# A sum of two matrix blocks moved from VectorE to two DMA transfers, and earlier places for an eigensolver's products

## The chip, the core and the metric

The kernel runs on one core of one Trainium2 chip. The core has five engines with a queue each: TensorE (PE, matrix products, with its weight loads shown as PEld), VectorE (DVE), ScalarE (ACT), GpSimd (POOL) and SyncE (SP). In the kernel before, nearly all DMA transfers are issued from SP and a few from ACT; none is issued from GpSimd. The metric is the device time of one execution in microseconds (us); lower is better.

## The reference, cut to what matters

The program is a stack of four graph layers on an input of 8192 rows of 256 numbers (128 graphs of 64 nodes), all in float32, each with a residual and a layer norm. Two of them matter here.

```python
# layer 0: three graph convolutions with one 64x64 matrix (adj * S, and S is adj)
def _slconv(x, adj, S, W):
    support = jnp.einsum('bnf,fh->bnh', x, W)
    weighting = adj * S
    return jnp.einsum('nm,bmh->bnh', weighting, support)
h = relu(_slconv(x, adj, S, W1))      # W1: 256 x 512
h = relu(_slconv(h, adj, S, W2))      # W2: 512 x 1024
y = _slconv(h, adj, S, W3)            # W3: 1024 x 256

# layer 1: needs the eigenvectors of a 64x64 Laplacian
_, U = jnp.linalg.eigh(L_norm)
agg = jnp.einsum('mn,bnd->bmd', U.T, features)
```

Layers 2 (LSTMs over windows of nodes) and 3 (attention) follow; the change does not touch them.

## The kernel before, in words

**Two stages.** In the first, `layer0` (line 1116) runs layer 0 over 16 groups of four row tiles (512 rows). In the same stretch `eigen` (line 275) finds the eigenvectors of the one 64x64 Laplacian. In the second stage a planner (`Plan`, line 104) lays out layers 1 to 3. Layer 1 needs the eigenvectors, in the tiles `u2` and `ut2`, so no product of the second stage can start before `eigen` has ended.

**Products by Strassen's way.** The second and third weights' products are made of 2x2 blocks with seven products in place of eight (`seven`, line 1056; it yields after each product). The order of the products is 1, 2, 6, 5, 7, 3, 4. For the third weight the inputs are the four blocks `H11`, `H12`, `H21`, `H22` of the tile `h2` (each 128 partitions x 4 x 256 numbers, 512 KB) and sums of them (lines 998 and 999): product 1 reads `H11`, product 2 reads `H12`, product 6 reads `sh[:, 1]`, product 5 reads `sh[:, 0]`, product 7 reads the new `H21`, product 3 reads the new `H12`, and product 4 reads `H22`. Four operations of VectorE make the sums (lines 1141, 1142, 1147 and 1148): `sh[:, 0]` is `H21 + H22`; `sh[:, 1]` is that less `H11`; then `H21` and `H12` are overwritten. In the program they stand behind product 2. Between product 2 and product 6 stand four products of the next group with the first weight (`weigh`, line 1091, called for t = 0 to 3), which do not need the sums; the last group has none, since no group follows.

**An order written out by hand.** PE, DVE and ACT take their instructions in the order in which the program gives them (the `manual_schedule` at line 1161); SP's and POOL's are placed by the framework. The eigensolver is a generator that is advanced between products of layer 0 (`between`, line 953). It has a clock of its own: `now` counts what PE has been given (in `mm`, line 963, some 0.22 us for a product with 128 columns, 0.43 with 256, 0.86 with 512), and `Timed` (line 42) adds up what VectorE has been given in `free`: 0.25 us for an instruction and 0.0009 us for each element of a partition beyond 64. Layer 0's own sums go through the same clock, by `VL` (line 1001). The eigensolver yields the time at which it wants to go on. There are two such times:

```python
def soon():
    return max(free[0], until[0]) - 0.45
def full(turns=0):
    return max(free[0], until[0]) + 0.3 + 0.6 * turns
```

Ahead of vector work it waits for `soon`, ahead of a product on PE for `full`; `until` is when the product before will be there (0.5 us after it was given, line 314). What is not yet given when layer 0 ends is given at once behind it (lines 1169 to 1171).

**What the eigensolver does.** It reduces the matrix to tridiagonal form in 62 Householder steps (lines 382 to 448), each with one product on PE (`mm(pq, L, AQ)`, line 415) behind a `full`; it finds the eigenvalues by bisection (lines 562 to 593), the vectors by recursions (lines 603 to 641), and then turns them, fixes their signs and multiplies (lines 642 to 752), with seven further places behind a `full` or a wait of that kind, each the start of a chain PE, DVE, PE.

**Around the change.** Product results are added by DVE or copied by ACT one product later (`step`, line 1005). The layer norm of a group is made in pieces in the next group (`scalar_norm`, line 800), with three small POOL instructions to each half, and is then stored by a 512 KB transfer from SP (line 1105). When the second weight `aw2` and the third, `aw3`, have been read for the last time, the weights of the later layers are loaded in their places from SP (lines 878 and 1203).

Of the kernel before, what the change touches and what calls it, by code (L numbers as in the profile page):

```python
# [13 lines left out]
ALU = mybir.AluOpType  # L14
# [260 lines left out]
def eigen(tc, stack, a, ident, cst, u2, ut2, now, free):  # L275
# [9 lines left out]
    nc = tc.nc  # L285
    until = [0.0]
# [6 lines left out]
    def sb(shape, tag):  # L293
        uid[0] += 1
        return wp.tile(shape, F32, tag=tag, name=f"{tag}_{uid[0]}")
# [10 lines left out]
        return max(free[0], until[0]) - 0.45  # L306

    def full(turns=0):
        return max(free[0], until[0]) + 0.3 + 0.6 * turns

    def mm(out, lhsT, rhs):
        PE.matmul(out, lhsT, rhs, start=True, stop=True)  # L312
# [37 lines left out]
    V.tensor_scalar(dm, C["eye"], y, None, op0=ALU.mult)  # L350
    pm = ps([N, N], "pa")
    yield full(4)
    mm(pm, m, dm)

# [9 lines left out]
    A, QT = AQ[:N, 0, :], AQ[:N, 1, :]  # L364
    S.copy(LV[0][:N, 1, :], eye[:, 0:1].to_broadcast([N, N]))
    yield full()


# [13 lines left out]
    for i in range(N - 2):  # L382
# [16 lines left out]
        for update in late[1:]:  # L399
# [11 lines left out]
                               op1=ALU.mult, accum_out=v)  # L411
        V.tensor_copy(L[:N, 0, :], v.to_broadcast([N, N]))
        yield full()
        pq = ps([W, 2, N], "pa")
        mm(pq, L, AQ)
# [187 lines left out]
    for k in range(1, N):  # L603
        c = N - 1 - k
        t = sb([W, 1], "tw")
# [223 lines left out]
def kernel(  # L829
# [25 lines left out]
    nc = tc.nc  # L855
# [32 lines left out]
    def rows_of(g):  # L888

        return X[:, 4 * g:4 * g + 4, :] if g < RING else XA[:, 4 * (g - RING):4 * (g - RING) + 4, :]  # L890
# [99 lines left out]
    sh = pa.tile([P, 2, 4, 256], F32, name="sh")  # L990
    s3 = pa.tile([P, 4, D], F32, name="s3")
    A11, A12, A21, A22 = (m2[:, k:k + 2, r:r + 256] for r in (0, 256) for k in (0, 2))
    H11, H12, H21, H22 = (h2[:, c:c + 4, r:r + 256] for r in (0, 256) for c in (0, 4))
# [6 lines left out]
    free = [0.0]  # L1000
    VL = Timed(V, free, now)
# [3 lines left out]
    def step(then=None):  # L1005

        while pending:
            pending.pop(0)()
        if then:
            pending.append(then)  # L1010
        if norms:
            norms.pop(0)()
# [4 lines left out]
    def sums_of_weights(w, b12):  # L1017
        VL.tensor_sub(w[7], w[3], b12)
        VL.tensor_sub(w[5], b12, w[1])
        VL.tensor_sub(w[6], w[3], w[5])  # L1020
        VL.tensor_sub(w[4], w[2], w[6])

    def burst(dst, src, c):
        to = dst.rearrange("p c (t h n) -> p h c t n", h=2, n=N)
        p = [bank().rearrange("p (c t n) -> p c t n", c=2, t=4) for _ in range(2)]
        for t in range(4):
            for k in range(2):
                for m, f, h, hs in quads(c + k):
                    PE.matmul(p[h][m, k, t, :], src[hs, t, f], sqT2[hs, hs], start=True, stop=True)  # L1029
        now[0] += QUADS  # L1030
        between()

        def result():
            for h in range(2):
                S.copy(to[:, h, c:c + 2], p[h])  # L1035

        step(result)
# [6 lines left out]
    def by_second(j):  # L1044

        def product(out, i, new):
            w, a = (x[i] for x in second)
            chained(out, [[(w[:, k, c * P:(c + 1) * P], a[:, k, :]) for k in range(2)] for c in (2 * j, 2 * j + 1)], new)

        return product  # L1050
# [5 lines left out]
    def seven(n, product, c11, c12, c21, c22, last):  # L1056

        def view(b):
            return b[:, :2 * n].rearrange("p (i n) -> p i n", i=2)

        def add(dst, b):
            VL.tensor_add(dst, dst, b)
            if last is relu:
                relu(dst, dst)

        ch = view(bank("ch"))
        product(ch, 1, True)
        step(lambda: S.copy(c11, ch))
        yield
        b2 = view(bank())  # L1070
        product(b2, 2, True)
        step(lambda: add(c11, b2))
        yield
        product(ch, 6, False)
        step(lambda: S.copy(c12, ch))
        yield
        b5 = view(bank("b5"))
        product(b5, 5, True)
        step(lambda: S.copy(c22, b5))
        yield  # L1080
        product(ch, 7, False)
        step(lambda: add(c22, ch))
        yield
        product(b5, 3, False)
        step(lambda: add(c12, b5))
        yield
        product(ch, 4, False)
        step(lambda: last(c21, ch))
        yield

    def weigh(t):
        p = bank()
        run(p, [(m1[:, k, t * P:(t + 1) * P], aw1[:, k, :]) for k in range(2)])
        step(lambda: relu(h1[:, t, :], p))

    def mix_rows(g, t):
        p = bank().rearrange("p (t f) -> p t f", t=2)
        mm(p, sqT2, s3[:, t:t + 2, :])

        def result():  # L1100
            x2 = rows_of(order[g])[:, t:t + 2, :]
            VL.tensor_add(x2, p, x2)
            norms.extend(scalar_norm(tc, small, x2, half, spare))
            if t and order[g] >= RING:
                norms.append(lambda: nc.sync.dma_start(rest[order[g]], rows_of(order[g])))

        step(result)

    def sums_second():
        S1, S2, S4 = (ss[:, i] for i in range(3))  # L1110
        VL.tensor_add(S1, A21, A22)
        VL.tensor_sub(S2, S1, A11)
        VL.tensor_sub(A21, A11, A21)
        VL.tensor_sub(S4, A12, S2)

    def layer0():
        n = NT // 4
        burst(m1, rows_of(order[0]), 0)
        step()
        for t in range(4):  # L1120
            weigh(t)
        step()
        sums_of_weights(second[0], B12)
        for c in (0, 2):
            burst(m2, h1, c)
        step()
        for g in range(n):
            sums_second()
            for j in range(2):
                q = [h2[:, 4 * c + 2 * j:4 * c + 2 * j + 2, r:r + 256] for r in (0, 256) for c in (0, 1)]  # L1130
                for _ in seven(256, by_second(j), *q, relu):
                    pass
                if j == 0 and g + 1 < n:
                    burst(m1, rows_of(order[g + 1]), 0)
                if j == g == 0:
                    sums_of_weights(third[0], D12)
            q = [s3[:, r:r + 2, c:c + P] for r in (0, 2) for c in (0, P)]
            w3 = seven(P, by_third, *q, S.copy)
            next(w3)
            next(w3)  # L1140
            VL.tensor_add(sh[:, 0], H21, H22)
            VL.tensor_sub(sh[:, 1], sh[:, 0], H11)
            for t in range(4):
                if g + 1 < n:
                    weigh(t)
                if t == 0:
                    VL.tensor_sub(H21, H11, H21)
                    VL.tensor_sub(H12, H12, sh[:, 1])
            for _ in range(4):
                next(w3)  # L1150
            if g + 1 < n:
                burst(m2, h1, 0)
            next(w3)
            if g + 1 < n:
                burst(m2, h1, 2)
            for t in (0, 2):
                mix_rows(g, t)
        step()

    eig.extend([0.0, eigen(tc, phase_a, adst[:N, :], ident, eig_c, u2, ut2, now, free)])  # L1160
    with tc.manual_schedule(engines={mybir.EngineType.PE, mybir.EngineType.DVE, mybir.EngineType.Activation}):
        pt = bank()
        PE.transpose(pt[:N, :P], adst, ident)
        for h in range(2):
            hs = slice(h * N, (h + 1) * N)
            V.tensor_copy(adT2[hs, hs], pt[:N, hs])
        V.tensor_mul(sqT2, adT2, adT2)
        layer0()
        while eig:
            now[0] = max(now[0], eig[0])  # L1170
            between()
# [562 lines left out]
```

## Time and profile before

| | |
|---|---|
| time, 3 runs | 2320.1 us median (2317.26, 2320.21, 2320.1) |
| the profiled execution's own time | 2317.55 us |
| its span, first to last instruction | 2315.7 us |
| PE / PEld / DVE / ACT / POOL busy over the span | 97% / 86% / 75% / 52% / 6% |
| first stage | 0 to some 845 us, the second from there |
| one group of layer 0, from one to the next | 50.5 us |
| the four sums of one group on DVE | 1.21 us (three of them) and 1.22 us |

Times in the trace are counted from the span's first instruction. A row of the timeline gives the start, the busy time, the engine, the line, the operation, what it writes and reads (out<-in), and how many instructions were merged in it; in brackets stands how long the engine sat idle before it and what ended the wait. Names of tiles are cut at a digit: `h` is `h1` or `h2`, `m` is `m1` or `m2`, `aw` is any of the first layer's weights. L52 is the line in `Timed` that gives the eigensolver's vector instructions and layer 0's own, L964 is `mm` of layer 0, L312 that of the eigensolver, L162 the planner's. PE carries a float32 product as two records, so that eight products count x16. A row of a table of windows gives the stretch, its length, each engine's busy time with its number of instructions, the granted clock of PE as a share of full speed, the busy share of the DMA engines, and GB/s. Ends of products are modelled, and overlap with the next one's start.

### The profile page before, as it was taken

The numbers are of one execution on the slowest core, as the hardware profiler recorded it, in microseconds if no ns is written. First come the engines' busy times: TensorE is split into PE (matmuls) and PEld (weight loads), VectorE is DVE, ScalarE is ACT, GpSimd is POOL, SyncE is SP. The second block draws the span as 40 slices with busy tenths as digits, with TensorE's granted clock in tenths as the row PEclk, the third lists the DMA queues.
The fourth block names the chain that finished last, engine by engine and source line by source line (L and its number), as shares of the span: only waits on it lengthen the run. The fifth ranks groups of instructions, "written<-read, shape, count | busy, mean of one in ns | idle before, by whom it ended". The sixth has DMA issues, their size and how long they took to land.

```text
span 2315.7 us, 51333 instructions
## 1 busy us (share of the span) xinstructions
PE 2247.0 (97%) x20228; PEld 1988.2 (86%) x20228; DVE 1744.2 (75%) x5718; ACT 1200.2 (52%) x2896; POOL 137.8 (6%) x315
## 2 busy tenths in 40 slices
PE   8999999999999969999999999999999999999996
PEld 6788888878888858999999999899899899998895
DVE  5887877777888978665957967867867776868764
ACT  3444444443444425665656655555655655655654
POOL 0000000000000010000100100100000010000001
PEclk9999999999999989999999999999999999999998
DMA  7000000000000031000201221211211220312300
GB/s 241 11 10 11 10 11 12 18 10 10 11 10 1 13 124 43 20 1 19 87 27 47 76 65 40 76 67 47 76 56 49 67 74 23 112 58 92 99 19 19
DMA packets 80114, 107.88 MB, mean 47 GB/s; under 512 B 23296, under 2 KB 64256, under 8 KB 79872
## 3 DMA queue, kind: packets, MB, share of 16 engines
q1 hardware_dynamic: 79520, 104.32, 14.1%
q8 instruction: 159, 2.61, 0.5%
q14 instruction: 83, 0.68, 0.1%
q10 hardware_dynamic: 352, 0.28, 0.0%
HBM read 57.64 MB, written 45.09 MB: 44 GB/s over the span
## 4 chain that ended last, share of the span: by engine, by line
PE 87%; DVE 8%; issue 1%; ACT 1%; DMA 1%; POOL 1%; SPq 0%; ACTq 0%; DVEq 0%; POOLq 0%
PE ps L162 55%; PE ch L964 13%; PE ps L964 9%; PE b L964 7%; PE ps L1029 2%; DVE X L162 1%; DVE w L162 1%; PE pa L312 1%; POOL rs L162 1%; DVE st L162 1%; DVE D L52 1%; DVE gates L162 1%; DVE tw L52 1%; ACT gates L162 1%; DVE w L52 0%
## 5 line engine op out<-in xcount | busy, mean ns | idle before, releaser
L162 PE MATMUL ps<-w,wih 128*128 128x128 f32 (+2 forms) x2944 | 572.9, 298 | 5.5 <-DVE gates L162 4.9
L162 PEld LDWEIGHTS ps<-w,wih 128*128 128x128 f32 x2944 | 454.5, 191 | 39.8 <-issue 13.5
L162 PE MATMUL ps<-w,sums 128*128 128x128 f32 (+2 forms) x3104 | 476.9, 294 | 5.8 <-DVE w L162 5.2
L162 PEld LDWEIGHTS ps<-w,sums 128*128 128x128 f32 x3104 | 419.8, 191 | 23.4 <-DVE w L162 6.6
L162 ACT ACTIVATE gates<-gates,cbi 128x256 f32<-128x256 f32 (+4 forms) x736 | 315.7, 482 | 189.1 <-DVE gates L162 186.3
L162 DVE TENSOR_TENSOR gates<-gates,ps 128x512 f32<-128x512 f32 (+4 forms) x408 | 236.7, 585 | 190.3 <-PE ps L162 182.0
L162 ACT COPY gates<-ps 128x512 f32<-128x512 f32 (+4 forms) x408 | 205.7, 509 | 238.7 <-PE ps L162 233.4
L162 PE MATMUL ps<-hs,whh 128*128 128x128 f32 (+1 forms) x896 | 182.2, 285 | 2.3 <-DVE hs L162 2.3
L162 PE MATMUL ps<-w,whh 128*128 128x128 f32 (+1 forms) x896 | 181.1, 284 | 0.0
L162 PEld LDWEIGHTS ps<-hs,whh 128*128 128x128 f32 x896 | 140.6, 193 | 2.5 <-DVE hs L162 2.5
L162 ACT ACTIVATE gates<-ps,cbi 128x128 f32<-128x128 f32 (+2 forms) x368 | 119.8, 387 | 41.8 <-PE ps L162 39.3
L162 PEld LDWEIGHTS ps<-w,whh 128*128 128x128 f32 x896 | 139.7, 191 | 0.0
L973 ACT ACTIVATE h<-h 128x512 f32<-128x512 f32 x96 | 60.6, 632 | 138.1 <-DVE h L52 138.1
L964 PE MATMUL ch<-m,tw 128*128 128x256 f32 x512 | 121.9, 381 | 3.6 <-DVE h L52 3.5
L964 PE MATMUL b<-ss,aw 128*128 128x256 f32 x512 | 122.9, 379 | 0.0
L964 PE MATMUL ps<-aw,m 128*128 128x512 f32 x256 | 115.2, 601 | 1.5 <-DMA aw<-in_a_w_dram 1.5
L964 PEld LDWEIGHTS ch<-m,tw 128*128 128x128 f32 x512 | 96.4, 190 | 19.4 <-DVE h L52 6.0
L964 PEld LDWEIGHTS b<-ss,aw 128*128 128x128 f32 x512 | 96.4, 190 | 12.6
L162 POOL TENSOR_SCALAR rs<-mv 128x2 f32<-128x2 f32 x96 | 26.1, 280 | 1352.1 <-DVE mv L162 1350.8
L964 PEld LDWEIGHTS ps<-aw,m 128*128 128x128 f32 x256 | 47.7, 193 | 54.8 <-issue 52.2
L1035 ACT COPY m<-ps 128x512 f32<-128x512 f32 x96 | 51.4, 588 | 76.3 <-PE ps L1029 75.9
L162 PE MATMUL ps<-hs,sums 128*128 128x128 f32 (+1 forms) x448 | 90.6, 284 | 0.0
(359 smaller groups left out, 4101.6 us busy)
## 6 DMA issues: line engine op xcount, KB each, us to landing
far<-w SPq DMA_DIRECT2D x42, 512.0 KB, 2.8
w<-far SPq DMA_DIRECT2D x168, 128.0 KB, 3.2
X<-rest SPq DMA_DIRECT2D x24, 512.0 KB, 3.6
out_dram<-X SPq DMA_DIRECT2D x64, 128.0 KB, 1.8
rest<-XA SPq DMA_DIRECT2D x12, 512.0 KB, 2.6
rest<-X SPq DMA_DIRECT2D x12, 512.0 KB, 2.7
XA<-in_x_dram SPq DMA_DIRECT2D x22, 256.0 KB, 6.7
aw<-in_a_w_dram SPq DMA_DIRECT2D x3, 1024.0 KB, 10.2
```

The lines of the kernel that those rows point to most:

```text
L52: return getattr(self.engine, name)(out, *args, **kw)
L162: getattr(e, name)(*[real(x) for x in args], **{k: real(v) for k, v in kw.items()})
L312: PE.matmul(out, lhsT, rhs, start=True, stop=True)
L964: PE.matmul(out, lhsT, rhs, start=start, stop=stop, **kw)
L973: S.activation(dst, src, AF.Relu)
L1029: PE.matmul(p[h][m, k, t, :], src[hs, t, f], sqT2[hs, hs], start=True, stop=True)
L1035: S.copy(to[:, h, c:c + 2], p[h])
```

## The change

The sum `sh[:, 0] = H21 + H22` is taken off VectorE: behind product 1, SP is given a transfer that copies `H22` to `sh[:, 0]`; behind product 2, GpSimd is given a transfer that adds `H21` to what stands there. The other three operations remain on VectorE, but all of them now stand behind the third of the four products with the first weight (t = 2), where before one stood ahead of these four and two behind the first of them (t = 0). In `full` the extra wait of 0.3 us is left out, so that the planner's clock gives the eigensolver's products to PE earlier.

```diff
     def full(turns=0):
-        return max(free[0], until[0]) + 0.3 + 0.6 * turns
+        return max(free[0], until[0]) + 0.6 * turns
...
             w3 = seven(P, by_third, *q, S.copy)
             next(w3)
+            nc.sync.dma_start(sh[:, 0], H22)
             next(w3)
-            VL.tensor_add(sh[:, 0], H21, H22)
-            VL.tensor_sub(sh[:, 1], sh[:, 0], H11)
+            nc.gpsimd.dma_start(sh[:, 0], H21, accum_op=ALU.add)
             for t in range(4):
                 if g + 1 < n:
                     weigh(t)
-                if t == 0:
+                if t == 2:
+                    VL.tensor_sub(sh[:, 1], sh[:, 0], H11)
                     VL.tensor_sub(H21, H11, H21)
                     VL.tensor_sub(H12, H12, sh[:, 1])
```

## The prediction

> **What bounds the kernel now.** I read the windows over the trace first, then the timeline of one group engine by engine, then the last group, then the transfers' rows of the page.
>
> ```profile
> 408.10:458.60 50.50, 50.50 (x450) 42.09 (x449) 39.38 (x189) 22.78 (x60) 2.16 (x6) 1.00 0.03 12
> 826.60:844.90 18.30, 2.23 (x12) 1.27 (x11) 14.65 (x84) 1.60 (x7) 1.20 (x3) 0.55 0.59 236
> ```
>
> The first row is one whole group of layer 0: PE is busy for all of its 50.5 us, DVE for 39.4. So in the groups PE is the bound, and a vector instruction saved there gains nothing by itself. The second row is the stretch between layer 0's last product and the first of layer 1: 18.3 us in which PE does 2.23 us of work while DVE runs 84 short instructions one behind the other. This is the end of the eigensolver, which wasn't given in time to lie under layer 0, and it is what the change can win: each microsecond by which the eigensolver moves ahead in the queues comes off this stretch until it is used up.
>
> The price must be looked for at the sums. Group 7, on ACT, DVE and PE:
>
> ```profile
> 405.80 0.63 ACT L973 ACTIVATE h<-h 128x512 f32<-128x512 f32 x1 [1.49 <-DVE h L52]
> 407.31 0.63 ACT L973 ACTIVATE h<-h 128x512 f32<-128x512 f32 x1 [0.87 <-DVE h L52]
> 408.31 0.60 ACT L973 ACTIVATE h<-ch 128x512 f32<-128x512 f32 x1 [0.37 <-PE ch L964]
> ```
>
> ```profile
> 411.43 1.21 DVE L52 TENSOR_TENSOR sh<-h 128x1024 f32<-128x1024 f32 x1
> 412.68 1.22 DVE L52 TENSOR_TENSOR sh<-sh,h 128x1024 f32<-128x1024 f32 x1
> ...
> 417.79 0.19 DVE L52 COPY LV<-u 64x64 f32<-64x64 f32 x1
> ```
>
> ```profile
> 411.90 7.03 PE L964 MATMUL ps<-aw,m 128*128 128x512 f32 x16
> 418.77 1.72 PE L964 MATMUL ch<-tv,sh 128*128 128x128 f32 x14
> 420.33 0.39 PE L312 MATMUL pa<-AQ,LV 128*128 128x128 f32 x2
> ```
>
> The three ACT rows finish H22 (at 406.43), H12 (407.94) and H21 (408.91). PE does the four first-weight products from 411.90 and needs sh[:, 1] at 418.77, for product 6; before, that was ready at 413.90, 4.9 us early. The last two rows on LV and pa show a Householder step's vector ready at 417.98 and its product at 420.33: 2.35 us of slack. Over the 62 steps I took the same difference; the least is 1.16 us.
>
> The last group has no first-weight products as cover, and meets the loads of the next layers:
>
> ```profile
> 811.36 1.95 PE L964 MATMUL ps<-aw,h 128*128 128x128 f32 x16
> 815.17 2.02 PE L964 MATMUL ch<-tv,sh 128*128 128x128 f32 x16 [1.86 <-DVE sh L52]
> ```
>
> ```profile
> 807.07 0.90 SPq L1203 DMA_DIRECT2D wih<-in_c_ih_dram  x2
> 808.03 0.45 SPq L878 DMA_DIRECT2D wih<-in_c_ih_dram  x1
> ```
>
> ```profile
> far<-w SPq DMA_DIRECT2D x42, 512.0 KB, 2.8
> rest<-XA SPq DMA_DIRECT2D x12, 512.0 KB, 2.6
> ```
>
> There PE already waits 1.86 us for the sums. The loads issued at 807 to 808 land by 814.75. The page's last two rows price a plain 512 KB transfer from SP at 2.6 to 2.8 us, issue to landing.
>
> **What the Trainium skill says.** "DMA: Bandwidth & Descriptors", "Anatomy of one DMA — SWDGE (gpsimd) path": a transfer issued from GpSimd costs about 2.0 us fixed plus its bytes at 436 GB/s, so 3.2 us for 512 KB. No run here shows one; the SP transfers of the trace (2.6 us) are near it. "Collectives: The Full Stack", "The bandwidth ceiling: the fold count and why AG ≠ RS ≠ AR": an adding transfer reads two sources, and its data rate measured half that of a copy. The trace has none. "SBUF — State Buffer", "SBUF: two separate sides": GpSimd's descriptor writing is locked out while DVE runs in a two-port mode (a transfer of 620 ns took 3100 ns there). DVE is 78% busy here, so this counts on the high side. "TensorE: Matmul & The Clock Gate", "What's actually happening": an idle window of about 3.4 us halves PE's clock. The trace agrees: 0.55 in the second window above.
>
> **The change part by part.** The sum is made against the profiled execution, 2317.55 us (span 2315.7); the runs' median, 2320.1, lies 2.55 us above it.
>
> *The sum off DVE.* 16 instructions of 1.21 us leave DVE, 19.4 us; none was on the path in groups 0 to 14. On the planner's clock each was worth 0.25 + 0.0009 x 960 = 1.11 us, so the eigensolver is given 16 x 1.11 = 17.8 us sooner by the end.
>
> *full without 0.3.* 62 Householder steps and 6 other places stand ahead of the tail. At the six, product and vector work alternate, and each gains 0.3: 1.8 us. In a Householder step 24 vector instructions of 0.25 make 6.0 us. Six of these follow the product without needing it, so a product given 0.3 sooner often only waits. Six steps (36 us) and layer 0's own vector work (13.5 us on the clock) make 49.5 of the group's 50.5: the clock is bound by vector work, not by the products. I take 4 of the possible 18.6 us and keep 0 and 18.6 for the range. Cost: a product that comes before its vector would stall PE, but 0.3 is less than the least slack of 1.16 us: nothing, and with that cover gone at most 62 x 0.3 = 18.6.
>
> *What the tail loses.* The tail is some 80 vector instructions (20 us of clock) and seven products with 0.7 us of lead each (4.9): 25 to 26 us with rounding. The advance is 17.8 + 1.8 + 4 = 23.6. So 2.4 us of clock stay behind, about 2 us of time (18.3 real for 26). The tail's products, 2.23 us at about half clock, move under PE's stream: some 1.3 us. The gain is -18.3 + 2 + 1.3 = -15.0. PE need not restart at half clock: products that took 4.0 us after 845 should take about 2.6, -1.4. DVE has room: it gives up 19.4 us and takes on 14.65.
>
> *The two transfers in groups 0 to 14.* The first waits for H22 (406.43), is given at 406.5 and lands 2.6 later at 409.1; H21 is there at 408.91. The second starts at 409.2. The sub of 1.22 us must start by 417.5 for product 6 at 418.77. So the second may take 8.2 us from its wait to its landing; 6.7 if the first is held until H12 is done (407.94). The sub's own place is behind t = 2, near 417.05 on PE, and DVE ran the sums 0.5 us ahead of PE's place, so order alone costs nothing. The duration isn't shown: low end 3.2 (a plain transfer), high end 10 (two reads, 2.0 + 2.4, then doubled for locks and for 1 KB pieces). I take 5.5: 4.4 for two reads and 1.1 for locks. That is hidden under product 1, product 2 and the first-weight products, and costs 0. Uncovered, each microsecond beyond 8.2 costs 15. No gain below zero is possible, as PE is full. Behind the waiting sub on DVE stand the eigensolver's instructions; late ones would hold PE's pa products only beyond the slack. SP carries the copy behind the group's store (issued at 404.24, landing 2.6 later), which shares the DMA engines for under 1 us. POOL's norm pieces of this group are over by 400.3, so the adding transfer queues behind nothing. Moving H21 and H12 behind t = 2 is free: they end near 420.5, product 7 starts at 422.57 and product 3 at 424.35.
>
> *The last group.* H22 is done at 808.36. The copy lands near 811.1 if SP gives it ahead of the weights' loads, as the program order has it. The adding transfer then shares the engines with those loads: 5.5 + 1.5 = 7, landing at 818.1; the sub ends at 819.4 against product 6 at 815.17. Cost +4.2, and +1.7 as PE, idle over 3.4 us, drops to half clock for a window. If cover is found (short transfer): +1. If the copy queues behind the loads (815): +8.
>
> *Sum.* -15.0 - 1.4 + 4.2 + 1.7 = -10.5, so 2307 in the profiled execution and 2309.6 beside the runs' median. I say 2310.
>
> **Rivals.** *The adding transfer is late.* Every group then stalls at product 6. With 10 us: (10 - 8.2) x 15 = 27, and 4.5 more in the last group; 2310 + 31.5, near 2341. Against it speaks 8.2 us of cover; for it, 1 KB pieces, locks, and that no such transfer is in the trace. It decides from 8.9 us, where 0.7 x 15 = 10.5 eats the gain. *The eigensolver stays locked to the groups.* The trace has exactly six Householder products in each of groups 1 to 9, with slacks that repeat from group to group, so its rounding to PE's steps may swallow the saved clock there. Then only the later 5.4 groups count: 5.4 x 1.11 + 1.8 = 7.8 of clock, 5.5 us of time; 5.9 go in the last group: near 2320. Against it: 1.1 us a group is more than the 0.4 to 1 us of rounding at hand. *All is hidden.* full gives most of its 18.6, the transfer takes 4 us: the tail is gone, the last group costs 1: -18.3 + 1.3 - 1.4 + 1 = -17.4, near 2303.
>
> **How the numbers follow.** Forecast 0.48 (2303 to 2316 by the last group's and the tail's ends); all hidden 0.10; locked 0.12; late transfer 0.30, from 2316 at 8.6 us to 2370 at 12. 0.2% (4.6 us) is about what a measurement of this kernel can tell. Below 2315.5: 0.46 + 0.10 = 0.56. Above 2324.7: most of the late case, 0.26, and 0.04 of the locked one: 0.30. Same: 0.14. The range reaches from 2301 to 2345: of the late case it leaves out transfers over 10.3 us, 0.13, and below 2301 some 0.04.
>
> **What would show it.** Right: PE busy between layer 0 and layer 1 with a gap under 4 us; DVE's wait for the adding transfer short; product 6 without a wait in groups 0 to 14 and a wait of about 6 us in the last. Wrong: PE waiting for sh in each group (then the transfer took over 8.2 us), six Householder products to a group as before, or a tail over 10 us.

## The result: slightly slower, and the profile after

The changed kernel took 2322.73 us (median of 12 runs, 2320.93 to 2328.06) beside 2318.76 us for the kernel before on the same chip (12 runs, 2315.39 to 2320.55): a ratio of 1.002, 95% interval [1.0011, 1.0028]. The profiled execution took 2320.93 us, with a span of 2319.2; before it was 2317.55 and 2315.7.

The stretch that was to be won has been won. This is the row of the windows over the changed kernel that answers to the second one shown of before; the columns are the stretch, its length, busy time (instructions) of PE, PEld, DVE, ACT and POOL, PE's clock, the DMA share and GB/s:

```profile
851.40:852.70 1.30, 0.83 (x12) 0.57 (x14) 1.24 (x5) 1.17 (x5) 0.00 (x0) 1.00 1.06 438
```

Layer 0 ends at 851.45 and layer 1's first product starts at 852.61: 1.16 us, where 18.9 lay before, and PE's clock is full. The profile's page also prices the two transfers, which are in no trace of before:

```profile
q0 software_dynamic: 8448, 8.39, 2.5%
...
sh<-h SPq DMA_DIRECT2D x16, 512.0 KB, 3.3
sh<-h POOLq DMA_DIRECT2D x16, 512.0 KB, 5.5
```

The copy from SP takes 3.3 us from issue to landing, the adding transfer 5.5, the value that the prediction took.

The loss is in the groups. The first row is a stretch of 50 us of the changed kernel:

```profile
205.00:255.00 50.00, 48.43 (x438) 39.77 (x438) 38.16 (x183) 22.32 (x59) 2.42 (x4) 1.00 0.13 33
```

PE is busy for 48.43 of 50 us; the same stretch of before has 50.00. What PE waits for between 60 and 800 us is told by the view of its waits (who waits, for whom: us in total, times, longest), first before, then after:

```profile
PE ch L964 <- DVE h L52: 2.0, 2, 1.6
```

```profile
PE ch L964 <- DVE h L52: 6.1, 9, 1.6
PE ch L964 <- ACT h L1075: 3.1, 6, 0.9
PE ch L964 <- DVE s L52: 0.2, 1, 0.2
```

None of these waits is for `sh` or for an eigensolver's vector. PE waits for additions and copies of the *second* weight's results. One case in the timeline of the changed kernel, near the end of group 2:

```profile
208.39 0.38 PE L312 MATMUL pa<-AQ,LV 128*128 128x128 f32 x2
...
208.81 0.26 DVE L52 SCALAR_TENSOR_TENSOR junk<-pa,q,xr 64x43 f32<-64x43 f32 x1 [1.07 <-PE pa L312]
...
211.04 0.26 DVE L52 SCALAR_TENSOR_TENSOR AQ<-xr,u,AQ 64x43 f32<-64x43 f32 x1
211.33 0.69 DVE L52 TENSOR_TENSOR h<-h,ch 128x512 f32<-128x512 f32 x1
...
212.07 1.99 PE L964 MATMUL ch<-m,tw 128*128 128x256 f32 x8 [1.57 <-DVE h L52]
```

The eigensolver's product (first line) falls at the end of product 7. Its vector instructions, one behind the other from 208.81 to 211.30, then stand on VectorE ahead of the addition of product 7's result (`h<-h,ch`). Product 4 writes the same tile `ch` and can't start before that addition has read it. Product 3, which takes 1.73 us from its start to the next one's, is all the cover there is. So PE waits 1.57 us. In the same way product 7 must wait until ScalarE has copied product 6's result out of `ch` (L1075); on ScalarE that copy stands behind the relu of product 2's result, which waits for VectorE's addition.

The account of the two profiled executions, stretch by stretch (a group runs from its first product with the third weight to the next group's):

| stretch | before | after | difference |
|---|---|---|---|
| start of the span to group 0 | 54.6 | 55.1 | +0.5 |
| groups 0 to 9 | 507.0 | 520.3 | +13.3 |
| groups 10 to 14 | 248.0 | 249.6 | +1.6 |
| last group, to layer 0's end | 16.5 | 26.5 | +10.0 |
| layer 0's end to layer 1's first product | 18.9 | 1.2 | -17.7 |
| the rest | 1470.8 | 1466.5 | -4.3 |

They add up to +3.4, the difference of the two executions. The time of a group, from its start to the next group's, is called its period. Before, groups 1 to 8 have 50.47 us each. After, groups 0 to 9 have 50.8, 53.55, 54.45, 51.12, 50.69, 52.12, 52.73, 50.94, 50.69 and 53.26: a pattern of four groups. In the trace of before, the eigensolver's six products of each of the groups 2 to 9 stand at the same six places; after the change 25 products fall in four groups, so that their places drift and come round after four. The long periods follow the places: in groups 1, 2, 5 and 6 an eigensolver's product falls into product 2 of the second weight, and others at the end of product 7 or into product 3, and these groups take 52.1 to 54.5 us; groups 0, 3, 4, 7 and 8, without a product in product 2, take 50.7 to 51.1.

In groups 10 to 14 the one long group is the last, with 52.81 us. PE waits there for a copy of ScalarE, 2.35 us, and the product behind the wait takes 3.25 us; the clock stands at 0.50 from 806.16 for 3.41 us.

The last group in the timeline of the changed kernel:

```profile
823.20 0.59 SPq L1140 DMA_DIRECT2D sh<-h  x1
823.89 1.62 SPq L1204 DMA_DIRECT2D wih<-in_c_ih_dram  x2
...
827.50 1.35 POOL L1142 DMA_DIRECT2D sh<-h  x1 [7.20 <-ACT s L1068]
...
835.95 1.23 DVE L52 TENSOR_TENSOR sh<-sh,h 128x1024 f32<-128x1024 f32 x1 [5.67 <-DMA sh<-h]
...
837.32 3.44 PE L964 MATMUL ch<-tv,sh 128*128 128x128 f32 x16 [8.13 <-DVE sh L52]
```

The copy is given ahead of the loads and lands at 826.79. The adding transfer is let go at 827.50 and lands at 835.93, 8.4 us later, beside loads that land from 828.16 to 833.23. PE waits 8.13 us and then does product 6 in 3.44 us where it took 2.02 before; the clock stands at 0.50 from 833.47 for 6.83 us.

### The profile page after: what moved, and what is told of

Its sections match the earlier page's. It is cut to its first block, busy times and chain, and to the rows that moved or that the text cites. A ratio compares the mean times of both kernels' runs of the same rounds, so it can differ in the third digit from the quotient of the medians.

```text
span 2319.2 us, 51447 instructions
## 1 busy us (share of the span) xinstructions
PE 2251.8 (97%) x20228; PEld 1986.2 (86%) x20228; DVE 1722.5 (74%) x5702; ACT 1194.6 (52%) x2896; POOL 159.7 (7%) x331
## 4 chain that ended last, share of the span: by engine, by line
PE 86%; DVE 9%; issue 1%; ACT 1%; DMA 1%; POOL 1%; SPq 0%; ACTq 0%; DVEq 0%; POOLq 0%
PE ps L162 55%; PE ch L964 13%; PE ps L964 9%; PE b L964 6%; PE ps L1029 2%; DVE X L162 1%; DVE w L162 1%; POOL rs L162 1%; DVE st L162 1%; DVE h L52 1%; PE pa L312 1%; DVE gates L162 1%; DVE D L52 1%; DVE tw L52 1%; ACT gates L162 1%
## 5 line engine op out<-in xcount | busy, mean ns | idle before, releaser
L964 PE MATMUL ch<-m,tw 128*128 128x256 f32 x512 | 127.1, 387 | 12.0 <-DVE h L52 6.5
L973 ACT ACTIVATE h<-ps 128x512 f32<-128x512 f32 x64 | 38.2, 597 | 95.0 <-PE ps L964 94.8
```

The lines of the kernel that those rows point to most:

```text
L964: PE.matmul(out, lhsT, rhs, start=start, stop=stop, **kw)
L973: S.activation(dst, src, AF.Relu)
```

## The experiments

Three theories stood at the start. **P**, the places: PE loses its time in the groups because the eigensolver's products, at other places, put their vector work ahead of additions that PE needs soon. **T**, the transfers: they, or the moved sums, hold VectorE or TensorE up. **F**: the shorter wait in `full` costs by itself. All ratios below are to the kernel before, which ran on the same chip beside each. The chips differ, so two of these runs are best compared by their ratios, and parts of the kernel by the periods.

**The transfers alone**: the changed kernel with `full` as before.

```diff
-        return max(free[0], until[0]) + 0.6 * turns
+        return max(free[0], until[0]) + 0.3 + 0.6 * turns
```

> Both transfers and the moved subs as in the changed kernel, but full keeps its 0.3 us. Theory P (places: with the sum off VectorE's account the eigensolver is no longer in step with the groups, its vector work falls ahead of layer 0's own sums, and PE waits at products 7 and 4 of the second weight): still out of step, groups 1 to 9 at 51 to 54 us each as in the changed kernel; part of the tail back, 5 to 8 us; some 3 to 8 us slower than the changed kernel. Theory T (transfers: the copying and adding themselves slow the groups): groups also at 51 to 54, but no slower than the changed kernel but for the tail. Theory F (the missing 0.3 us is the cause): groups back at 50.5 us, 10 us faster than the changed kernel.

2335.91 us, ratio 1.008 [1.0066, 1.0093]. Groups 0 to 9 took 527.5 us, with periods up to 55.76; 6.5 us of the gap between the layers were left; product 6 of the last group waited 8.79. PE's waits are again those behind the additions (60 to 800 us):

```profile
PE ch L964 <- DVE h L52: 9.5, 11, 1.7
PE ch L964 <- ACT h L1075: 5.1, 7, 1.1
PE ch L964 <- DVE sh L52: 0.5, 1, 0.5
```

So `full` isn't what costs; leaving the 0.3 out makes this kernel better, by 13 to 14 us.

**full alone**: the kernel before with only the first edit of the change.

```diff
-        return max(free[0], until[0]) + 0.3 + 0.6 * turns
+        return max(free[0], until[0]) + 0.6 * turns
```

> Only full loses its 0.3 us, the four sums stay on VectorE at their old places. Theory P: the eigensolver stays in step, six products to a group, and the tail shortens by 1 to 2 us: within 2 us of the kernel before. Theory T: the same. Theory F: groups lengthen to 51 to 54 us, 13 us slower than before.

2313.15 us, ratio 0.9982 [0.9974, 0.999]: faster than before. Groups 0 to 9 took 506.4 us, each from 50.46 to 50.69 but for group 9. The eigensolver stays in step with the groups, six products to most, at places that are harmless. The gap between the layers keeps 18.2 us. F falls. The gain of 4 us is more than the 2 expected; 2.6 us of it lie in the rest of the program, which differs by as much between other runs.

**The transfers, with the eigensolver's order held as it was before**: the clock is charged for the four sums where it was charged before, and the three that remain are given uncounted.

```diff
             nc.gpsimd.dma_start(sh[:, 0], H21, accum_op=ALU.add)
+            charge(2)
...
+                if t == 0:
+                    charge(2)
                 if t == 2:
-                    VL.tensor_sub(sh[:, 1], sh[:, 0], H11)
-                    VL.tensor_sub(H21, H11, H21)
-                    VL.tensor_sub(H12, H12, sh[:, 1])
+                    V.tensor_sub(sh[:, 1], sh[:, 0], H11)
+                    V.tensor_sub(H21, H11, H21)
+                    V.tensor_sub(H12, H12, sh[:, 1])
```

(`full` has its 0.3, and `charge(k)` adds the price of k sums to `free`.)

> Transfers and moved subs as in the changed kernel; full keeps 0.3 us, and the kernel's own clock is charged for four sums at the old places, so that the eigensolver's instructions stand where they stood before. Theory P: groups 1 to 9 at 50.5 us as before, the tail of 18 us is back, product 6 of the last group waits some 8 us: 6 to 8 us slower than before, near 2325. Theory T: groups at 51 to 54 us besides: 18 to 21 us slower than before, near 2338.

2335.34 us, ratio 1.0078 [1.0066, 1.0091]. This one didn't decide as hoped. The eigensolver's products stand at the places of before, and groups 0 to 9 fell from 527.5 to 511.3, most of the way to the 507 of before, as P has it; but groups 10 to 14 rose to 254.8, and new waits came up:

```profile
PE ch L964 <- DVE s L52: 3.4, 4, 1.2
PE pa L312 <- DVE LV L52: 2.2, 3, 1.2
```

The sums are now given later than the clock believes, and PE waits for VectorE at two new places, for the vectors `LV` and for the third weight's results. With the full gap (18.9 us) and the last group's 8.89 us of waiting the total is near what T had expected. So a part of T holds in this kernel: the moved sums can cost where the clock doesn't count them where they stand.

**Without the transfers**: the changed kernel with neither of them. `sh[:, 0]` holds a constant; the sum is left out.

```diff
-            nc.sync.dma_start(sh[:, 0], H22)
...
-            nc.gpsimd.dma_start(sh[:, 0], H21, accum_op=ALU.add)
```

> The changed kernel without its two transfers: the sum of H21 and H22 is left out, a constant stands in its place, everything else is where it was. Theory P: groups 0 to 9 as long as in the changed kernel (520 us in all), the last group's wait falls from 8 to about 1 us: 7 to 9 us faster than the changed kernel, near 2315. Theory T: groups back at 50.5 us, 13 us more: near 2302.

2314.18 us, ratio 0.9989 [0.9981, 0.9997]. The periods of groups 0 to 9 are those of the changed kernel within 0.02 us (sum 520.3), and the waits are the same to the digit:

```profile
PE ch L964 <- DVE h L52: 6.1, 9, 1.6
PE ch L964 <- ACT h L1076: 3.1, 6, 0.9
PE ch L964 <- DVE s L52: 0.2, 1, 0.2
```

The transfers cost nothing in groups 0 to 13. In the last they cost 7.2 us (19.25 in place of 26.45, product 6 waiting 2.37). Group 14 took 51.11 in place of 52.81, but the 1.7 us aren't the transfers': the wait of 2.35 us is there in both, and only the speed behind it differs. First the changed kernel, then this run:

```profile
805.58 3.25 PE L964 MATMUL ch<-m,tw 128*128 128x256 f32 x8 [2.35 <-ACT h L1075]
```

```profile
805.73 1.99 PE L964 MATMUL ch<-m,tw 128*128 128x256 f32 x8 [2.35 <-ACT h L1076]
```

In this run the clock stays at 1.00 there. The run shown next, which has the transfers in group 14, takes 51.11 us for it as well. What is left of T, the three moved sums, is still in this run; the run with an uncounted sum, further below, is without them.

**The last group's sum on VectorE again**, all else as changed:

```diff
+            if g + 1 < n:
-            nc.gpsimd.dma_start(sh[:, 0], H21, accum_op=ALU.add)
+                nc.gpsimd.dma_start(sh[:, 0], H21, accum_op=ALU.add)
+            else:
+                VL.tensor_add(sh[:, 0], H21, H22)
```

(The copy is left out there too, and the three sums stand at their old place in that group.)

> The changed kernel, but in the last group the sum is made by VectorE at its old place. If the 10 us lost in the last group come from the two transfers there (the copy lands 3.6 us after it is given, the adding transfer 8.4 us after it was let go, and TensorE then runs a window at half clock), product 6 waits 1 to 3 us again and the last group takes some 17 us in place of 26.5: about 8 to 9 us faster than the changed kernel, near 2314, with the periods of groups 0 to 9 unchanged at a sum of 520. If the last group's wait had another cause (vector work that now stands ahead there), it stays over 6 us and the time stays near 2322.

2317.57 us, ratio 1.0006 [0.9998, 1.0014]: 3 us better than the changed kernel by the ratios and 5 by the medians, not 8 to 9. The last group took 20.7 us, still 4.2 more than before. The timeline says why:

```profile
825.43 0.33 PE L312 MATMUL pa<-eig_c,bc 64*64 64x64 f32 x2
...
827.86 1.21 DVE L52 TENSOR_TENSOR sh<-h 128x1024 f32<-128x1024 f32 x1
829.10 1.22 DVE L52 TENSOR_TENSOR sh<-sh,h 128x1024 f32<-128x1024 f32 x1
...
830.47 0.90 PE L964 MATMUL ch<-tv,sh 128*128 128x128 f32 x5 [3.62 <-DVE sh L52]
```

A product of the eigensolver's end now falls into this group, and its eight vector instructions (825.80 to 827.94) stand ahead of the sum. Product 6 waits 3.62 us and then takes 3.25. It is P's mechanism again, at another place.

**The additions ahead of the eigensolver's work**: the direct trial of P. The changed kernel, in which the second weight's additions of products 2 and 7 are given to VectorE right behind their product, and with them the relu that follows on ScalarE.

```diff
         product(b2, 2, True)
         step(lambda: add(c11, b2))
+        if last is relu:
+            pending.pop(0)()
...
         product(ch, 7, False)
         step(lambda: add(c22, ch))
+        if last is relu:
+            pending.pop(0)()
```

> The changed kernel with one thing different: for the second weight, VectorE's additions of the results of products 2 and 7 are given right behind their product and not one product later, so they stand ahead of the vector instructions of an eigensolver's product that falls in the next one. The eigensolver's products stay at the changed kernel's places, within 1 us. Theory of the places, as I hold it: TensorE lost its 13 us in groups 0 to 9 because products 7 and 4 waited for these additions behind 11 Householder instructions; then the sum of groups 0 to 9 falls from 520 to 507 to 511 and the time to about 2311 to 2314. Rival: the places cost because Householder products themselves come too early for their vectors, or because of contention that has nothing to do with the additions; then the sum stays at 518 or more, and it grows if the additions, waiting for their product, hold the Householder chain up.

2309.25 us, ratio 0.9966 [0.9953, 0.9978]: 12 to 13 us better than the changed kernel by this one move. Groups 0 to 9 took 509.3 (50.82 52.46 50.95 50.47 50.69 50.47 50.77 50.47 50.69 51.49), and PE's waits for those additions are gone. Of those for the copy of product 6's result (L1077 here) 1.8 of 3.1 us are left over this window:

```profile
PE ch L964 <- ACT h L1077: 1.8, 3, 0.9
PE ch L964 <- DVE sh L52: 0.8, 1, 0.8
PE ch L964 <- DVE s L52: 0.5, 1, 0.5
PE ch L964 <- ACT h L1068: 0.5, 1, 0.5
```

VectorE does stand still for an addition that waits for its product, and it does no harm:

```profile
206.05 0.69 DVE L52 TENSOR_TENSOR h<-h,ch 128x512 f32<-128x512 f32 x1 [0.90 <-PE ch L964]
206.66 0.25 DVE L52 SCALAR_TENSOR_TENSOR junk<-pa,q,xr 64x43 f32<-64x43 f32 x1
...
207.73 1.89 PE L964 MATMUL ch<-m,tw 128*128 128x256 f32 x8
```

It is the same place in the same group as the case shown of the changed kernel: the addition now comes first, the Householder instructions behind it, and product 4 has no wait. P is shown for 11 of the 13.3 us.

**Both of these edits**:

> Both of these edits together. If the two losses are independent, 13 and 8 us come off the changed kernel: about 2302 to 2306, faster than both kernels, with a gap of some 1 us between layers 0 and 1, groups 0 to 9 at 507 to 511 and product 6 of the last group waiting 1 to 3 us. If the rival holds for the groups, 2314 as with the last group's sum alone.

2304.59 us, ratio 0.9948 [0.9936, 0.9961], faster than both kernels. Groups 0 to 9 509.3, the last group 20.8, the gap between the layers 2.9.

**The same additions in the kernel before**, to see whether that edit is a gain by itself:

> The kernel before with only the two additions given right behind their product, as in the run of the changed kernel that had this edit. The kernel before has one wait of TensorE for such an addition in groups 0 to 9 (1.6 us). Theory of the places: the edit cures waits that only the new places bring, so here it gains that 1.6 us at most: 2315 to 2317, with the tail of 18 to 19 us between layers 0 and 1. Rival: the edit is a gain of its own, whatever the places; then this kernel is 5 us or more faster than before, and the changed kernel's own part in the gain is small.

2320.51 us, ratio 1.0017 [1.001, 1.0024]: not a gain, and slightly slower. Groups 0 to 9 took 505.1 (1.9 less), the last group 3.4 more (product 6 waits 3.17 in place of 1.86), the gap 0.8 more, and the start of the span to group 0 1.3 more. So the additions' early places are worth 12 to 13 us at the changed kernel's places of the eigensolver's products and nothing at those of before: 2309.25 us stand against 2320.51 with that edit in both.

**Transfers only where no Householder step is left** (groups 10 to 14), VectorE's sums elsewhere, `full` without 0.3:

```diff
+            by_dma = 10 <= g < n - 1
+            if by_dma:
+                nc.sync.dma_start(sh[:, 0], H22)
...
+            if by_dma:
+                nc.gpsimd.dma_start(sh[:, 0], H21, accum_op=ALU.add)
+            else:
+                VL.tensor_add(sh[:, 0], H21, H22)
+                VL.tensor_sub(sh[:, 1], sh[:, 0], H11)
```

> The kernel before with the 0.3 left out of full, the four sums on VectorE in groups 0 to 9 and in the last, the two transfers only in groups 10 to 14, where no Householder step is left. On the kernel's own clock the eigensolver stays in step with the groups, at places that cost nothing with the full edit alone, and 14.5 us of it are left behind layer 0 (23.9 with the full edit alone). Theory of the places: groups 0 to 9 stay near 506.4, the tail falls from 18.2 to some 11, and the time is 2306 to 2309. Rival: the moved sums and the transfers cost by themselves wherever they stand; then groups 10 to 14 take 252 or more in place of 248 and the time is at or above 2313.

2312.61 us, ratio 0.9979 [0.9971, 0.9988]. Groups 0 to 9 506.4 and 10 to 14 247.8, as expected. The gap fell to 11.75, as expected, though the kernel's own clock leaves 17.8 us behind layer 0 when it is worked through, not the 14.5 of the expectation. But the last group took 18.8 us, where `full` alone had 15.8. Product 6 waits 2.15 us in place of 0.84, and behind this wait it is slow; the second line is the run without transfers:

```profile
816.06 3.43 PE L964 MATMUL ch<-tv,sh 128*128 128x128 f32 x16 [2.15 <-DVE sh L52]
```

```profile
830.03 2.02 PE L964 MATMUL ch<-tv,sh 128*128 128x128 f32 x16 [2.37 <-DVE sh L52]
```

The shorter wait was followed by 3.41 us at a clock of 0.50 (from 816.42), the longer one by none. The rest took 4.4 us more than with `full` alone, which isn't explained. So it is level with `full` alone, above the forecast.

**Which part breaks the step**: `full` without 0.3, all four sums on VectorE at their old places, but one of them not counted on the clock. No transfer, nothing moved.

```diff
-            VL.tensor_add(sh[:, 0], H21, H22)
+            V.tensor_add(sh[:, 0], H21, H22)
```

> The kernel before with the 0.3 left out of full and the sum H21 + H22 made by VectorE at its old place, but not counted on the kernel's own clock (1.11 us less of it in each group); no transfer and nothing moved. If it is the missing 1.11 us a group that breaks the step between eigensolver and groups, the places drift over four groups as in the changed kernel, groups 0 to 9 take 515 to 524, the tail is gone (gap under 4 us) and the last group has no wait over 4 us: some 2314 to 2320. If the step holds without the moved operations, groups 0 to 9 stay at 507 and the tail at 16 to 18: near 2313.

2318.42 us, ratio 1.0005 [0.9997, 1.0013]. Groups 0 to 9 took 519.5, in the pattern of the changed kernel (50.8 53.54 54.44 50.47 50.69 52.12 53.78 50.47 50.69 52.49), and the gap is 1.2. With `full` alone the step held. So the gain of the gap and the loss in the groups both come with 1.11 us a group less on the clock by which the code orders itself, and the moved sums aren't needed for the loss; that VectorE was relieved of a sum has little part in it.

**The same with the additions placed early**:

> The same with the two additions of the second weight's results given right behind their products. No DMA transfer is in it: VectorE still makes all four sums, so it has 1.21 us a group more to do than its clock counts. If VectorE's freed time is worth nothing and only the places and the additions count, groups 0 to 9 take 508 to 512 and the time is 2302 to 2308, level with the version that has the transfers in groups 0 to 14. If the transfers' relief of VectorE is needed, the groups take 515 or more and TensorE waits for LV or sh in them.

2305.39 us, ratio 0.9954 [0.9938, 0.9969]: level with both edits together (2304.59), with no DMA transfer added at all. Groups 0 to 9 509.9; VectorE's extra work shows in group 14, where PE waits 2.78 us for a third-weight result, and groups 10 to 14 take 250.9 where that version takes 248.3.

## Why the prediction was wrong, step by step

**PE bounds the groups, and the stretch between the layers is what can be won**: right. The gap went from 18.9 to 1.16 us. The forecast took 18.3 away and left 2.

**The advance, 17.8 + 1.8 + 4 = 23.6 us**: right in size. On the kernel's clock 25.7 us of eigensolver were left at layer 0's end before, and 1.5 after. What gives it is the counting, as the run with an uncounted sum shows.

**The transfers in groups 0 to 14**: right. The adding transfer took 5.5 us as taken, the copy 3.3 where 2.6 was taken, and both are hidden. The Trainium skill's price ("DMA: Bandwidth & Descriptors", "Anatomy of one DMA — SWDGE (gpsimd) path") makes an estimate of 3.2 us for a plain transfer of this size; with the add it is 5.5. That the total came out doesn't show its parts: no run here tells 4.4 us for two reads from 1.1 for locks, so the hit is in part luck. (The high end of 10 doesn't follow from its sum: 4.4 doubled is 8.8.) No long stretching by locks is seen: with VectorE at 76% (38.16 of 50 us) the transfers outside the last group took 5.4 to 5.9.

**"so the eigensolver is given 16 x 1.11 = 17.8 us sooner by the end", with no cost set against it**: here it failed. The move of the eigensolver in the queues was counted as a gain alone; what its new places cost stood at 0 without a reason, and it was +13.3 us in groups 0 to 9. I measured the slack of those who wait for the *eigensolver's* vectors and that of product 6, and never asked who waits *behind* the eigensolver's vector instructions in VectorE's queue. Those are the second weight's additions, with a single product of 1.73 us as cover ahead of products 7 and 4. The kernel before had the Householder products at six fixed places, and there these additions came in time (one wait of 1.6 us in groups 0 to 9); I took the repeating slacks of its trace only as a sign of how fast the eigensolver would go on, not as a condition that the change would break. The trial with the additions first takes 11 of the 13.3 away.

The idle times before PE's products in these groups show only 7.6 of the 13.3 (9.2 in place of 1.6). In the trace, some 5 us more lie in the product ahead of a wait and in the one behind it, which are drawn longer (1.99 us in place of 1.89 behind it). Some 2 us lie in two products that take 0.1 us more in each group, with the additions first too; why isn't shown.

The two costs of order that the prediction did look at were rightly put at nothing. "0.3 is less than the least slack of 1.16 us": `full` alone lost nothing in the groups (506.4 against 507.0), and no eigensolver's product waits for its vector in the changed kernel's view. (The 1.16 us is counted to the weight load; to the product itself, as in the case shown, the least is 1.38.) "so order alone costs nothing": with all sums at their old places the groups still took 519.5.

**The last group, +4.2 + 1.7**: right mechanism, too small. The stretch grew by 10.0; 1.3 of that was forecast as the tail's products moved under PE, so 8.7 stands against 5.9. The adding transfer took 8.4 us beside the loads and not 7, the copy 3.6 and not 2.7; product 6 waited 8.13 where 6.1 followed from the working. The Trainium skill ("TensorE: Matmul & The Clock Gate", "What's actually happening") has an idle window of about 3.4 us halve the clock. The trace agrees for this long wait: 3.44 us for product 6 behind 8.13 us of idling, against 2.02. But 3.4 us of idling isn't a limit below which one is safe: a wait of 2.15 us was followed by half clock, and one of 2.37 us was not. Taking the transfers out doesn't give the whole back (with the last group's sum on VectorE it took 20.7 against 16.5), as the eigensolver's end now stands ahead of the sum there: the same omission as above.

**Restart at full clock, -1.4**: sign right. The rest of the program lost 4.3 us. Over all runs it takes 1463.2 to 1468.4 us where the gap is under 3 us and 1467.3 to 1472.6 where it is longer, so the size can't be told closely from single profiles.

**Against the forecast's sum**: -10.5 was forecast, +3.4 came. The 13.9 between them are 13.3 (groups 0 to 9), 1.6 (10 to 14, where 1.7 came from a stretch at half clock in group 14), 2.8 (last group), 0.5 (start), -1.4 (gap) and -2.9 (rest).

**The rivals**: the late transfer (the sum waits in every group) is refuted by the run without transfers; the eigensolver isn't locked to the groups either, since the places drift. The slower case that came true was none of those that I had set out, and of the signs set down nearly all of those for being right came up (a gap under 4 us, product 6 without a wait in groups 0 to 14) while the time rose.

## What to carry to other kernels

In a queue that is ordered by hand, an instruction's place has two sides: who waits for it, and who stands behind it. Before moving a chain in time, list the consumers with the thinnest cover (here two additions with one product to hide them) and see whether the chain can now fall in front of them; a pattern that repeats exactly from group to group may be what protects them. Where a planner's clock orders the code, find out whether a change acts through the engines or through the clock: here one uncounted sum on VectorE did the same as two DMA transfers.

## What was not expected of the hardware

An adding transfer of 512 KB within SBUF took 5.5 us from its wait to its landing with quiet queues, and 8.4 us beside the weights' loads; its instruction kept GpSimd busy for 1.33 us. A plain copy of 512 KB within SBUF took 3.3 us from SP, where stores of that size took 2.6.

Whether TensorE's clock fell after a wait didn't follow from the length of the wait: after 2.15 us it fell to 0.50 for 3.41 us, after 2.37 us in another run it stayed at 1.00, and after 2.35 us at the same place in two runs it fell in one and not in the other. Each such stretch cost some 1.2 to 1.7 us, which is not small beside some of the differences compared here.
